# Adding the last norm's shift in a transfer instead of on GpSimd, with three output tiles and a shorter gate lead

## The chip, the core and the metric

The kernel runs on one core of a Trainium2 chip. The metric is the device time of one execution in microseconds (us). All data is float32.

## What is computed

The input `x` has 384 rows of 384 positions with 128 channels. Two layers follow each other:

```
# layer 0, a triangle product
z     = layernorm(x)
left  = (z @ Wl + bl) * sigmoid(z @ Wlg + blg)
right = (z @ Wr + br) * sigmoid(z @ Wrg + brg)
core  = einsum('bikh,bjkh->bijh', left, right)
x1    = x + sigmoid(x @ Wg + bg) * (layernorm(core) @ Wout + bout)
# layer 1, gated rows
left  = x1 @ W_left + b_left + x1 @ W_eq + b_eq
gate  = sigmoid(x1 @ W_gate + b_gate)
rsum  = sum over a row's 384 positions of (x1 @ W_right + b_right)
out   = (left * rsum * gate) @ W_out + b_out
y     = layernorm(out + x1) * ln_scale + ln_bias
```

The change concerns the very last step, `+ ln_bias`.

## The kernel before

**Three stages.** Stage 1 normalises `x`, makes `left` and `right` and writes them to a scratch tensor in DRAM. Stage 2 takes one channel `h` at a time, multiplies `left` by `right` on TensorE and writes `core_d`. Stage 3 does all that is left of layer 0 and the whole of layer 1, row by row. Stages 1 and 2 are not touched by the change.

**Slots of stage 3.** The loop runs over `t`, here called slot `t`, from 0 to 393, and each engine works through its own queue in program order. Row `i` passes through the slots as through a pipeline: in slot `i` GpSimd multiplies the core row by its scale (`cs`, L446); in slot `i+2` TensorE applies `Wout` (`pr`, L473) and VectorE forms `x1T` (L474, L476); in slot `i+3` come the two products `pg` and `pl` (L489, L490) and `u`; in slot `i+6` the row sums of four rows (`pq`, `rsum`, L463 to L465); in slot `i+7` the output product `py` (L505, L506), its statistics on VectorE (L511, L513) and, for two rows at a time, the power on GpSimd (`rs`, L515 to L520); in slot `i+9` ScalarE applies mean and scale (L527). In slot `i+10` (`D = 10`) VectorE multiplies by `-ln_scale` into the output tile `yt` (L454), which is the first VectorE instruction of its slot, and GpSimd adds `ln_bias` in place (L457).

**Quads.** An output tile holds four rows (`RG = 4`), a quad, here named by its first row. There are two output tiles (pool `p3out`), so the first L454 of quad `i+8` waits until the store of quad `i` has landed. Stores go out on SyncE's queue (SP) after the last row of a quad (L554); the last four rows are stored one by one (L549), 192 KB each instead of 768 KB.

**Fronts and their lead.** `front(f)` transposes the four tiles of row `f` of `x` (`pxt`, L431) and computes the gate of row `f-2` (`pg`, L423). Fronts run ahead of the slots:

```
while f < min(N + 2, t + max(2, A - t // 3)):
    if f == 6:
        rstd()
        load_core(0)
        load_core(RG)
    front(f)
```

With `A = 16`, sixteen fronts run before slot 0, and the lead then shrinks by one in every third slot until it is 2, in slot 42. While it shrinks, two slots in three hold a front. After that every slot holds one. `rstd()` (L395 to L414) turns the sums of stage 2 into the core's scale, writes it to DRAM and reads it back broadcast to all partitions (`rt`, L389); slot 0 needs it, and the fronts before slot 0 keep TensorE busy meanwhile.

**SyncE's queue.** All loads of stage 3 and all stores go through SP in program order. `front(f)` with `f` a multiple of 4 begins with the load of rows `f+16` to `f+19` into one of four tiles (L382): that tile holds rows `f` to `f+3`, so SP stands still until TensorE has transposed row `f+3`. In every slot that is a multiple of 4, `load_core` (L387, L389) follows, and a store L554 of quad `i` comes at the end of slot `i+13`. All of them stand behind L382 in the queue.

Of the kernel before, what the change touches and what calls it, by code (L numbers as in the profile page):

```python
# [8 lines left out]
F32 = mybir.dt.float32  # L9
AF = mybir.ActivationFunctionType  # L10
ALU = mybir.AluOpType
# [3 lines left out]
P = 128  # L15
# [4 lines left out]
def triangle_then_gated_row_kernel(ctx: ExitStack, tc: tile.TileContext, a: dict, out: bass.AP):  # L20
# [9 lines left out]
    nc = tc.nc  # L30
    x = a["x"].rearrange("b i j c -> (b i) j c")
    y = out.rearrange("b i j c -> (b i) j c")
    N, _, C = x.shape
    H = a["L0_conv_Wl"].shape[1]
    assert C == P and H == P and N % P == 0
    NB = N // P
# [2 lines left out]
    XR = 8  # L39
    KEEP = 2  # L40
    RG = 4
    A = 16

    cpool = ctx.enter_context(tc.tile_pool(name="const", bufs=1))
    dpool = ctx.enter_context(tc.tile_pool(name="scratch", bufs=1, space=DRAM))
# [4 lines left out]
    def seq(ins):  # L50

        return tc.keep_in_program_order(ins)

    def const(shape, name):
        return cpool.tile(shape, F32, tag=name, name=name)
# [18 lines left out]
    with ExitStack() as ctx2:  # L74
        lrp = ctx2.enter_context(tc.tile_pool(name="lr", bufs=2))
        inp = ctx2.enter_context(tc.tile_pool(name="p2in", bufs=3))
# [13 lines left out]
        with tc.tile_pool(name="p1x", bufs=6, side="right") as xp, \  # L90
# [71 lines left out]
            lns, lnb = const([P, C], "lns"), const([P, C], "lnb")  # L162
# [65 lines left out]
            def front(z):  # L228

                pt = tps.tile([P, 4, P], F32, tag="pt", name="pt")  # L230
                for r in range(4):
                    seq(nc.tensor.transpose(pt[:, r, :], z[:, r, :], ident))  # L232
                zt = wp.tile([P, 4, P], F32, tag="zt", name="zt")
                seq(nc.scalar.copy(zt, pt))  # L234
                return zt
# [74 lines left out]
        with tc.tile_pool(name="p2out", bufs=2, side="right", reuse_waits="tile") as op, \  # L310
# [23 lines left out]
            for h in range(H):  # L334
                fill(h + 1)
                t, rr = loaded2.pop(h), right.pop(h)
# [23 lines left out]
    with ExitStack() as ctx3:  # L360
        def pool(name, bufs, **kw):
            return ctx3.enter_context(tc.tile_pool(name=name, bufs=bufs, reuse_waits="tile", **kw))

        xip, fp, inp, op = pool("p3x", 4), pool("p3f", A + 4), pool("p3in", 3), pool("p3out", 2)
        wp, lp, sp = pool("p3w", 4), pool("p3l", 7), pool("p3s", 4)
        ps, ps2 = pool("p3ps", 4, space=PSUM), pool("p3ps2", 4, space=PSUM)

# [6 lines left out]
        cols = [slice(b * P, (b + 1) * P) for b in range(NB)]  # L374
        lnsb = lns.unsqueeze(1).to_broadcast([P, NB, C])
        lnbb = lnb.unsqueeze(1).to_broadcast([P, NB, C])
        rows, yts, pair, quad, xin, cin = {}, {}, {}, {}, {}, {}

        def load_x(i0):
# [4 lines left out]
        def load_core(i0):  # L384
            if i0 < N:
                ct = inp.tile([P, RG, N], F32, tag="ct", name="ct")
                seq(nc.sync.dma_start(out=ct, in_=core_d[i0:i0 + RG].rearrange("i h j -> h i j")))  # L387
                rt = inp.tile([P, RG, N], F32, tag="rt", name="rt")
                seq(nc.sync.dma_start(  # L389
                    out=rt.rearrange("p i j -> p (i j)"),  # L390
                    in_=rstd_d[i0:i0 + RG].rearrange("i j -> (i j)").partition_broadcast(P),
                ))
                cin[i0] = ct, rt

        def rstd():  # L395


            def temp(tag, bufs):
                return rp.tile([P, N], F32, tag=tag, name=tag, bufs=bufs)

            w = [(temp("ve", NB), temp("r", NB)) for _ in range(NB)]
            for b, (ve, r) in enumerate(w):
                m = temp("m", 2)
                seq(nc.vector.scalar_tensor_tensor(m, csum[:, b], 1.0 / (H * H), csum[:, b], ALU.mult, ALU.mult))
                seq(nc.vector.scalar_tensor_tensor(ve, csq[:, b], 1.0 / H, m, ALU.mult, ALU.subtract))
                seq(nc.vector.tensor_scalar(ve, ve, 0.0, EPS, ALU.max, ALU.add))
                seq(nc.scalar.activation(r, ve, AF.Sqrt))
            for b, (ve, r) in enumerate(w):
                m = temp("m", 2)
                seq(nc.vector.reciprocal(m, r))  # L410
                seq(nc.vector.tensor_mul(r, m, m))
                seq(nc.vector.scalar_tensor_tensor(r, r, -0.5, ve, ALU.mult, ALU.mult))
                seq(nc.vector.scalar_tensor_tensor(r, r, 1.5, m, ALU.add, ALU.mult))
                seq(nc.gpsimd.dma_start(out=rstd_d[b * P:(b + 1) * P, :], in_=r))  # L414

        D = 10
# [19 lines left out]
        def tick(t):  # L436
# [5 lines left out]
            if r:  # L442
                i = t
# [4 lines left out]
            if r:  # L448

                i = t - D  # L450
                if i % RG == 0:
                    yts[i] = op.tile([P, RG, NB, C], F32, tag="yt", name="yt")
                yt = yts[i // RG * RG][:, i % RG]
                seq(nc.vector.tensor_tensor(  # L454
                    yt, r["py"][:, :N].rearrange("p (b c) -> p b c", b=NB), lnsb, ALU.mult
                ))
                seq(nc.gpsimd.tensor_tensor(yt, yt, lnbb, ALU.add))  # L457
            m, n = divmod(t - 6, 4)
            if n == 0 and m in quad:

# [73 lines left out]
        for t in range(N + D):  # L534
# [7 lines that stand above are left out]
                f += 1  # L542
            if t % RG == 0:
                load_core(t + 2 * RG)
            tick(t)
            i = t - D
            rows.pop(i, None)
            if i >= N - RG:
                seq(nc.sync.dma_start(  # L549
                    out=y[i].rearrange("(b p) c -> p b c", p=P), in_=yts[N - RG][:, i % RG]  # L550
                ))
            elif i >= 0 and i % RG == RG - 1:
                i0 = i - RG + 1
                seq(nc.sync.dma_start(out=y[i0:i0 + RG].rearrange("i (b p) c -> p i b c", p=P), in_=yts.pop(i0)))  # L554


# [27 lines left out]
```

## Time and profile before

| what | us |
|---|---|
| median of four runs | 3465.4 (3463.13 to 3467.33) |
| the profiled execution | 3467.31 |
| its span | 3465.5 |
| stage 1, from the span's start to the first `pc` matmul | 1149 |
| stage 2, to its last `pc` matmul | 743 |
| stage 3, to the end of the span | 1573 |

Busy time in the whole span: TensorE 3408.4 us (98%), VectorE 2421.6 us (70%), ScalarE 1948.1 us (56%), GpSimd 2341.2 us (68%). The profiled execution is the span and 1.8 us around it, and it is 1.9 us longer than the median. A busy TensorE is not TensorE at its peak: a matmul's busy time also shows the pace of the clock it was granted. A releaser in square brackets is what ended an engine's idle time ahead of the instruction.

### The profile page before, as it was taken

How to read it: one execution, taken by the hardware profiler on the slowest of the kernel's cores; microseconds unless marked ns; L12 is line 12 of the kernel's file. 1: busy time of each engine (PE TensorE's matmuls, PEld its weight loads, DVE VectorE, ACT ScalarE, POOL GpSimd, SP SyncE). 2: the span in 40 equal slices, each digit the busy share in tenths (PEclk: the TensorE clock that was granted, in tenths of full speed). 3: DMA queues.
4: the chain of work that ended last, by engine and by line, in shares of the span. 5: the costliest groups of instructions: out<-in, count | busy, mean ns of one | idle time of the engine just before them, and what ended most of it. 6: DMA issues, size and time to landing. Idle time of an engine off the chain costs nothing.

```text
span 3465.5 us, 47967 instructions
## 1 busy us (share of the span) xinstructions
PE 3408.4 (98%) x13646; PEld 2107.5 (61%) x13646; DVE 2421.6 (70%) x7498; ACT 1948.1 (56%) x3815; POOL 2341.2 (68%) x4041
## 2 busy tenths in 40 slices
PE   8999999999999999999999989999999999999998
PEld 3444444444444566666665667777777777777775
DVE  5666666666666555555555778888888888888887
ACT  3344444444444333333334667777777777777776
POOL 6677777777777555555564567777777777777776
PEclk9999999999999999999999999999999999999999
DMA  3685866858765598999999655666666656565662
GB/s 95 193 232 163 230 197 198 233 162 229 199 195 151 184 284 282 282 282 284 283 284 279 200 186 186 194 200 201 196 205 192 209 188 212 185 213 187 210 210 83
DMA packets 884865, 726.00 MB, mean 209 GB/s; under 512 B 18533, under 2 KB 823017, under 8 KB 884601
## 3 DMA queue, kind: packets, MB, share of 16 engines
q1 hardware_dynamic: 882336, 720.31, 67.6%
q8 instruction: 110, 1.80, 0.2%
q10 hardware_dynamic: 2072, 2.04, 0.2%
q14 instruction: 155, 1.26, 0.1%
q0 software_dynamic: 192, 0.59, 0.0%
HBM read 437.07 MB, written 285.80 MB: 209 GB/s over the span
## 4 chain that ended last, share of the span: by engine, by line
PE 96%; DMA 2%; DVE 1%; POOL 1%; ACT 0%; issue 0%; SPq 0%; POOLq 0%; ACTq 0%; DVEq 0%
PE pr L255 29%; PE pc L340 21%; PE pr L473 7%; PE py L505 7%; PE pl L490 7%; PE pg L489 7%; PE pg L423 7%; PE pt L232 4%; PE py L506 3%; PE pxt L431 3%; DMA out_dram<-yt 1%; PE pq L463 0%; POOL rs L516 0%; DMA rt<-rstd_d 0%; ACT py L527 0%
## 5 line engine op out<-in xcount | busy, mean ns | idle before, releaser
L255 PE MATMUL pr<-wz,zt 128*128 128x512 f32 x2304 | 1040.8, 594 | 0.7 <-ACT zt L234 0.7
L340 PE MATMUL pc<-rr,lrh 128*128 128x384 f32 x2304 | 743.3, 486 | 1.5 <-issue 1.5
L257 ACT ACTIVATE sg<-pr 128x512 f32<-128x512 f32 x576 | 344.2, 598 | 645.6 <-PE pr L255 332.3
L255 PEld LDWEIGHTS pr<-wz,zt 128*128 128x128 f32 x2304 | 416.6, 191 | 415.1 <-issue 414.1
L259 DVE TENSOR_TENSOR lr<-pr,sg 128x512 f32<-128x512 f32 x576 | 398.5, 692 | 377.7 <-ACT sg L257 377.7
L340 PEld LDWEIGHTS pc<-rr,lrh 128*128 128x128 f32 x2304 | 451.8, 196 | 293.2 <-issue 2.3
L527 ACT ACTIVATE py<-py,nm,rs 128x128 f32<-128x128 f32 x1152 | 495.5, 430 | 124.3 <-POOL rs L520 94.6
L223 POOL TENSOR_SCALAR z<-xt,rs,sh 128x128 f32<-128x128 f32 x1152 | 497.6, 448 | 0.6 <-POOL z L223 0.4
L505 PEld LDWEIGHTS py<-wo,u 128*128 128x128 f32 x2304 | 378.7, 191 | 107.2 <-ACT py L527 3.2
L349 DVE TENSOR_TENSOR csum<-csum,ct 128x1152 f32<-128x1152 f32 x128 | 192.0, 1500 | 345.6 <-ACT ct L346 345.6
L505 PE MATMUL py<-wo,u 128*128 128x128 f32 x2304 | 404.4, 275 | 4.8 <-ACT py L527 3.0
L457 POOL TENSOR_TENSOR yt<-yt,lnb 128x384 f32<-128x384 f32 x384 | 383.3, 998 | 19.8 <-DVE yt L454 19.8
L346 ACT COPY ct<-pc 128x1152 f32<-128x1152 f32 x128 | 143.3, 1120 | 450.1 <-PE pc L340 446.2
L326 POOL COPY rr<-lrh 128x768 f32<-128x768 f32 x128 | 171.2, 1337 | 323.6 <-DMA lrh<-lr_d 284.3
L446 POOL TENSOR_TENSOR cs<-ct,rt 128x384 f32<-128x384 f32 x384 | 383.5, 999 | 7.8 <-PE pxt L431 3.8
L511 DVE BATCH_NORM_STATS2 st<-py 128x6 f32<-128x128 f32 x1152 | 266.6, 287 | 111.3 <-PE py L506 111.2
L423 PE MATMUL pg<-xT,mat_L_conv_Wg 128*128 128x384 f32 x768 | 314.8, 492 | 13.6 <-DVE rsum L465 8.9
L473 PE MATMUL pr<-cs,wc 128*128 128x384 f32 x768 | 320.2, 499 | 0.0
L490 PE MATMUL pl<-x1T,mat_L_conv_W_left 128*128 128x384 f32 x768 | 312.5, 489 | 2.4 <-DVE rsum L465 2.3
L506 PE MATMUL py<-ident,x1T 128*128 128x128 f32 x1152 | 314.6, 273 | 0.0
L489 PE MATMUL pg<-x1T,mat_L_conv_W_gate 128*128 128x384 f32 x768 | 312.3, 488 | 2.3 <-ACT gT L425 1.4
L474 DVE SCALAR_TENSOR_TENSOR pr<-pr,bz,gT 128x384 f32<-128x384 f32 x384 | 240.1, 625 | 106.5 <-PE pr L473 106.5
(88 smaller groups left out, 5040.3 us busy)
## 6 DMA issues: line engine op xcount, KB each, us to landing
lr_d<-lr SPq DMA_DIRECT2D x128, 1024.0 KB, 9.3
lrh<-lr_d SPq DMA_DIRECT2D x128, 768.0 KB, 7.7
xt<-in_x_dram SPq DMA_DIRECT2D x144, 512.0 KB, 7.0
xt<-in_x_dram SPq DMA_DIRECT2D x96, 768.0 KB, 5.0
ct<-core_d SPq DMA_DIRECT2D x96, 768.0 KB, 6.7
rt<-rstd_d SPq DMA_DIRECT2D x96, 768.0 KB, 8.2
out_dram<-yt SPq DMA_DIRECT2D x95, 768.0 KB, 9.2
core_d<-ct SPq DMA_DIRECT2D x125, 576.0 KB, 8.8
```

What stands on the lines that cost most here:

```text
L223: seq(nc.gpsimd.tensor_scalar(z[:, r, :], xt[:, rr, :], rs[:, rr:rr + 1], sh[:, rr:rr + 1], ALU.mult, ALU.add))
L255: seq(nc.tensor.matmul(pr[:, r, :], lhsT=zt[:, 2 * half + r, :], rhs=wz, start=True, stop=True))
L259: seq(nc.vector.tensor_tensor(t[:, :, i0:i0 + 2, :], pr[:, :, :2 * H].rearrange("k i (h s) -> k h i s", s=2), sg.rearrange("k i (h s) -> k ...
L340: seq(nc.tensor.matmul(pc[:, ib, :N], lhsT=t[:, kb, ib * P:(ib + 1) * P, 0], rhs=rr[:, kb], start=(kb == 0), stop=(kb == NB - 1),))
L423: seq(nc.tensor.matmul(pg[:, :N], lhsT=wg0, rhs=r["xT"], start=True, stop=True))
L446: seq(nc.gpsimd.tensor_tensor(cs, ct[:, i % RG], rt[:, i % RG], ALU.mult))
L473: seq(nc.tensor.matmul(pr[:, :N], lhsT=wc, rhs=r["cs"], start=True, stop=True))
L489: seq(nc.tensor.matmul(pg2[:, :N], lhsT=wgate, rhs=r["x1T"], start=True, stop=True))
L490: seq(nc.tensor.matmul(pl[:, :N], lhsT=wleft, rhs=r["x1T"], start=True, stop=True))
L505: seq(nc.tensor.matmul(py[:, s], lhsT=r["u"][:, s], rhs=r["wo"], start=True, stop=False))
L506: seq(nc.tensor.matmul(py[:, s], lhsT=r["x1T"][:, s], rhs=ident, start=False, stop=True, is_transpose=True))
L527: seq(nc.scalar.activation(py[:, s], py[:, s], AF.Identity, bias=nm[:, n, b:b + 1], scale=rs[:, n, b:b + 1]))
```

## The change

The add of `ln_bias` (L457) leaves GpSimd for all rows but the last four. In its place a constant tile `lnb4`, which holds `ln_bias` twelve times per partition, is filled once by GpSimd before stage 3 begins, and in slot `i+14` GpSimd's queue issues a transfer that adds `lnb4` to the whole output tile of quad `i` in place (`accum_op`). The store of quad `i` moves from slot `i+13` to slot `i+17`, and waits for that transfer. The output pool gets a third tile, and `lnb4` is as large as one of them; `A` falls from 16 to 12, which frees four tiles of each of the two kinds in pool `p3f`.

```diff
-    A = 16
+    A = 12
...
-        xip, fp, inp, op = pool("p3x", 4), pool("p3f", A + 4), pool("p3in", 3), pool("p3out", 2)
+        xip, fp, inp, op = pool("p3x", 4), pool("p3f", A + 4), pool("p3in", 3), pool("p3out", 3)
+        cp = pool("p3c", 1)
...
+        lnb4 = cp.tile([P, RG, NB, C], F32, name="lnb4")
+        seq(nc.gpsimd.tensor_copy(
+            lnb4.rearrange("p i b c -> p (i b) c"), lnb.unsqueeze(1).to_broadcast([P, RG * NB, C])
+        ))
...
-                seq(nc.gpsimd.tensor_tensor(yt, yt, lnbb, ALU.add))
+                if i >= N - RG:
+                    seq(nc.gpsimd.tensor_tensor(yt, yt, lnbb, ALU.add))
...
                 seq(nc.sync.dma_start(
                     out=y[i].rearrange("(b p) c -> p b c", p=P), in_=yts[N - RG][:, i % RG]
                 ))
-            elif i >= 0 and i % RG == RG - 1:
-                i0 = i - RG + 1
+            i0 = t - D - RG
+            if 0 <= i0 < N - RG and i0 % RG == 0:
+                seq(nc.gpsimd.dma_start(
+                    out=yts[i0].rearrange("p i b c -> p (i b c)"), in_=lnb4.rearrange("p i b c -> p (i b c)"),
+                    accum_op=ALU.add,
+                ))
+            i0 = t - D - RG - 3
+            if 0 <= i0 < N - RG and i0 % RG == 0:
                 seq(nc.sync.dma_start(out=y[i0:i0 + RG].rearrange("i (b p) c -> p i b c", p=P), in_=yts.pop(i0)))
```

## The prediction

> **What bounds the kernel.** I read the page's busy shares first (TensorE 98%), then busy time by stretches of stage 3. Columns: stretch, length, then busy time of TensorE, its weight loads, VectorE, ScalarE, GpSimd, then granted clock, DMA share, GB/s.
>
> ```profile
> 1930.00:2000.00 70.00, 66.07 (x327) 46.01 (x326) 53.12 (x188) 44.45 (x104) 43.52 (x62) 0.98 0.46 151
> 2000.00:2400.00 400.00, 391.24 (x1998) 279.06 (x1997) 321.22 (x1116) 294.38 (x680) 285.38 (x395) 0.99 0.60 194
> 2400.00:2800.00 400.00, 400.00 (x2071) 288.05 (x2069) 329.57 (x1136) 307.06 (x707) 291.23 (x406) 1.00 0.62 201
> 3420.00:3465.50 45.50, 28.61 (x154) 21.26 (x152) 27.37 (x106) 25.86 (x61) 28.22 (x42) 0.84 0.24 70
> ```
>
> From about 2095 to 3420 TensorE has no idle time: a quad takes 15.85 us (the chain's marks at 2412.18, 2428.03 and 2443.88), and GpSimd stands at 73%. So the adds that leave GpSimd (380 of 998 ns, 379 us) buy nothing there. What can move is the first 200 us of stage 3 and the last 30. The waits between 1880 and 2100 (total, times, longest) name the cause in the first part:
>
> ```profile
> DVE yt L454 <- DMA out_dram<-yt: 17.1, 5, 4.6
> PE pg L423 <- DVE rsum L465: 8.9, 3, 3.1
> PE pl L490 <- DVE rsum L465: 2.3, 2, 2.0
> ```
>
> VectorE waits five times for an output tile whose store has not landed; `rsum`, next in its queue, is late, and TensorE stands. TensorE's timeline (start, length, instruction, idle before it) has these five, and the start of slot 2:
>
> ```profile
> 1917.52 0.49 PE L431 MATMUL pxt<-ident,xt 128*128 128x128 f32 x3
> 1917.85 1.46 PE L473 MATMUL pr<-cs,wc 128*128 128x384 f32 x4
> ...
> 1977.75 0.91 PE L423 MATMUL pg<-xT,mat_L_conv_Wg 128*128 128x384 f32 x2 [2.94 <-DVE rsum L465]
> ...
> 2009.16 0.91 PE L490 MATMUL pl<-x1T,mat_L_conv_W_left 128*128 128x384 f32 x2 [0.33 <-DVE rsum L465]
> ...
> 2028.12 0.91 PE L423 MATMUL pg<-xT,mat_L_conv_Wg 128*128 128x384 f32 x2 [2.84 <-DVE rsum L465]
> ...
> 2059.80 0.91 PE L490 MATMUL pl<-x1T,mat_L_conv_W_left 128*128 128x384 f32 x2 [1.96 <-DVE rsum L465]
> ...
> 2079.00 1.65 PE L423 MATMUL pg<-xT,mat_L_conv_Wg 128*128 128x384 f32 x2 [3.09 <-DVE rsum L465]
> ```
>
> SP's queue shows why stores are late: each burst begins when L382 is released, and the store goes out behind it.
>
> ```profile
> 1996.60 0.37 SPq L382 DMA_DIRECT2D xt<-in_x_dram  x1
> 1997.07 0.70 SPq L387 DMA_DIRECT2D ct<-core_d  x1
> 1997.82 0.95 SPq L389 DMA_DIRECT2D rt<-rstd_d  x1
> 1998.87 0.48 SPq L554 DMA_DIRECT2D out_dram<-yt  x1
> ...
> 2019.22 0.37 SPq L382 DMA_DIRECT2D xt<-in_x_dram  x1
> 2019.69 0.71 SPq L554 DMA_DIRECT2D out_dram<-yt  x1
> ...
> 3453.77 0.37 SPq L554 DMA_DIRECT2D out_dram<-yt  x1
> ```
>
> **Step 1, what the five waits cost now.** From the lead's formula, front `f` runs in a known slot, so the release of each L382, and of the store behind it, is a slot number. With A = 16 the stores of quads 0, 8, 12, 20, 24 leave in slots 17, 23, 29, 35, 41, and their tiles are wanted in slots 18, 26, 30, 38, 42. These are the five waits. Idle: 2.94 + 0.33 + 2.84 + 1.96 + 3.09 = 11.2. After a gap TensorE may run slower: from 1977.75 the next five groups took 4.96 us, where the same groups take 2.93 at full pace, so 2.0 lost; 2079.00 to the `pr` at 2087.01 took 8.0, where a front (0.98) and a slot (3.91) make 4.9, so 3.1; by the same reckoning 0.5 after 2028.12 and 0.1 after 2059.80. Together 5.7. The waits cost 16.9 us.
>
> The granted clock shows it: 0.78 from 2070 to 2085. A gap of 2.94 us was enough for it and one of 2.84 nearly free. The Trainium skill ("TensorE: Matmul & The Clock Gate", Part 1) says that the clock halves after an idle window of about 3.4 us; by that rule all five gaps would cost their idle time alone, 11.2 us. The rows decide: 16.9.
>
> **Step 2, what is left of them.** With A = 12 every front of the shrinking lead comes in the slot in which the front four rows earlier came, and the lead reaches 2 in slot 30, not 42. The store of quad `i` is now queued in slot `i+17`, and its tile is wanted in slot `i+22`: both move by four slots, so the third tile by itself gives the store no more time. The same reckoning: quad 0 leaves in slot 17, wanted in 22 (free); quad 4 in 23, wanted in 26; quad 8 in 29, wanted in 30; from quad 12 on, five or four slots, as in the steady part, where there was no wait. Two waits remain.
>
> Slot 26 is the kind that cost 0.33 and 2.1. There the transfer of quad 8, issued in slot 22, runs beside the burst and holds up the store behind it by 2.5 to 4.9 us (step 4): 0.3 to 6, taken 4.5. Slot 30 is the kind that cost 3.3 (2.8 to 6 by the clock), taken 3.3. Left 7.8; gain 16.9 - 7.8 = **9.1 us** (4.9 to 13.8).
>
> **Step 3, the shorter lead.** TensorE's sixteen fronts ended at 1917.85, when `cs` of row 0 had been ready for over a microsecond:
>
> ```profile
> 1915.58 3.87 POOL L446 TENSOR_TENSOR cs<-ct,rt 128x384 f32<-128x384 f32 x4
> ```
>
> Four fronts fewer (0.98 each) end at 1913.95. `cs` begins after the scale's third write on GpSimd (1915.01), which A does not move, and takes 0.97. TensorE stands from 1913.95 to 1916.6: **2.65 us lost**, since the four fronts are made up later, in slots 30 to 42. Slow clock after it: by the gap of 2.84 up to 0.5, by that of 2.94 2.0. Taken 2.7, bounds 0 and 4.7. `lnb4`'s copy falls into GpSimd's idle 20.2 us before 1906.55; with 1.34 us for 768 elements (L326) it needs about 2.7 us, while VectorE's sums there have 3.2 us of waiting for ScalarE. Nothing; without that cover up to 2.7 us, all ahead of `rt`.
>
> **Step 4, the added transfer, steady part.** Per quad the DMA engines work 0.62 x 15.85 = 9.8 us for four transfers of 768 KB, 2.46 each; 6.0 are free. No accumulating transfer is in the trace. It moves as many bytes into the tile, so 2.46 is its floor, and since it must also read the tile I take twice that, 4.9, as upper bound and value. Both fit into 6.0.
>
> The Trainium skill ("Collectives: The Full Stack", on the fold count) says that a reducing transfer runs at half a copy's rate because of its two source reads. That speaks against the change; an estimate by that rule, two copies' time, would be no less than the value taken, and no row here shows it.
>
> The store in the burst now lands some 9.1 + 4.9 = 14 us after its issue, about 2.5 us behind the release, and its tile is wanted 18 to 20 us after the release: 2 to 3 us to spare. On GpSimd the issue costs about 0.56 us (L414, 0.54 to 0.80); behind it stand `cs` and the next `rs`, which idles 1.8 to 2.0 us before each pair, where 2 of 4 us of adds are gone too. SP's next loads stand behind the store's wait for the transfer, issued four slots earlier: nothing unless it takes over 15.85 us. Steady part: **0** (no gain, since TensorE is full).
>
> **Step 5, the end.** Before, the store of quad 376 left at 3453.77 and the last row's add ended at 3462.49; its 192 KB take 2.0, and the span ends at 3465.5, 1.0 later. Now quad 376's transfer is issued behind `rs` of the last pair (3458.16) and its 768 KB store is the very last instruction on SP. Issue by 3458.9; landing between 4.4 us (a 768 KB store here) and 8.8 (twice that), then 4.4 for the store and 1.0: 3468.7 to 3473.1, so +3 to +8, taken **+4.5**. A few adds fewer in the chain of the end give back below 0.5.
>
> **Sum.** -9.1 + 2.7 + 4.5 = -1.9 on the profiled 3467.3: 3465.4. The median is 1.9 below that execution, so **3463.5** there. The ends add up to -10.8 and +7.8: 3455 to 3473 is this case's own range.
>
> **Rivals.** *The waits go:* the transfer does not hold up the store in slot 26, quad 8 loses little, the end is short. 13.8 gained, 0 to 1 lost at the start, 3 at the end: about 3456. For it: both 0.33 and 2.1 stand in the trace. Against it: quad 8's store leaves one slot before it is wanted. 0.17. *The losses return:* slow clock at the start, 6 us at each wait, +8 at the end: 3473. 0.15. *The DMA engines fill:* above 6.0 us per transfer (2.4 times a copy) the burst no longer fits into a quad, stores land late in every quad, and TensorE waits for VectorE as in slot 18. At three times a copy (7.4) a quad grows by 1.4 us; 84 quads between 2100 and 3430 make +115, so 3580. For it: the DMA share is 0.62 already and the transfer reads twice. Against it: its rows are 6 KB long in each partition, while most packets here are below 2 KB. 0.20. *Nothing moves:* the waits shift by four slots and all come back: 3465. 0.04. My forecast has 0.44.
>
> **Chances.** 0.2% is 7 us, about what a measurement of this kernel tells from no change. Faster: nearly all of the first rival and the edge of the forecast, 0.19. Slower: the filled DMA engines, most of the returning losses and the edge, 0.36. Within: 0.45. The range 3453 to 3485 leaves out most of the filled engines (0.16) and little below.
>
> **What would show it.** Right: L454 waits twice for stores before 2100; TensorE idle about 2.6 us before the first `pr`; TensorE at 400.00 of 400 in the steady part with a DMA share of 0.8 to 0.95; the span ends with quad 376's store. Wrong: a quad longer than 15.85 us; L454 waiting for `out_dram` after 2200; five waits again.

## The result and the profile after

The changed kernel takes 3469.5 us (median of 42 runs, 3466.3 to 3472.4) against 3465.6 us (60 runs of the kernel before): a ratio of 1.0011, with a 95% interval of 1.0007 to 1.0015. It is 3.9 us slower, inside the forecast range and inside 0.2%, but on the other side of the forecast, which had 1.9 us faster. Its profiled execution has a span of 3469.2 us, 3.7 us longer than before.

Busy time by stretches of stage 3 (columns as before):

```profile
1930.00:2000.00 70.00, 69.02 (x350) 48.86 (x349) 57.71 (x205) 48.02 (x111) 34.67 (x52) 1.00 0.59 179
2400.00:2800.00 400.00, 399.96 (x2069) 287.85 (x2069) 329.56 (x1136) 306.56 (x707) 220.62 (x330) 1.00 0.86 250
3420.00:3469.20 49.20, 28.84 (x152) 22.09 (x150) 26.82 (x105) 25.42 (x61) 21.33 (x34) 0.79 0.56 137
```

The steady part is as forecast: TensorE is full, GpSimd falls from 73% to 55%, the DMA share rises from 0.62 to 0.86, and nearly every quad still takes 15.85 us. The waits from 1880 to 2110, and below the dots the one from 2110 to 3400:

```profile
DVE yt L459 <- DMA out_dram<-yt: 10.4, 3, 5.6
...
PE pl L496 <- DVE rsum L471: 4.8, 1, 4.8
...
PE pg L428 <- DVE rsum L471: 3.1, 1, 3.1
PE pr L479 <- POOL cs L451: 2.8, 1, 2.8
...
DVE yt L459 <- DMA out_dram<-yt: 4.5, 10, 0.6
```

Two waits that reach TensorE are left of five, in slots 26 and 30, as the slot numbers said. But they are larger than their forerunners. TensorE's timeline:

```profile
1895.55 1.65 PE L428 MATMUL pg<-xT,mat_L_conv_Wg 128*128 128x384 f32 x2 [1.02 <-ACT xT L438]
...
1918.59 2.59 PE L479 MATMUL pr<-cs,wc 128*128 128x384 f32 x4 [2.77 <-POOL cs L451]
...
2010.14 1.65 PE L496 MATMUL pl<-x1T,mat_L_conv_W_left 128*128 128x384 f32 x2 [4.81 <-DVE rsum L471]
...
2031.33 1.03 PE L428 MATMUL pg<-xT,mat_L_conv_Wg 128*128 128x384 f32 x2 [3.05 <-DVE rsum L471]
```

The gap in slot 26 was 0.33 us before and is 4.81 now, and the doubled times after it (1.65 for a pair that takes 0.81 to 0.91 at full pace) show the slow clock. Marks make the loss countable: the `pq` matmuls of slots 26 and 30 are 21.30 us apart, those of slots 30 and 34 are 20.93 apart. Without the waits (kernel `e5_after_load_late` below) the same stretches take 14.21 and 15.85. So the two cost 7.1 and 5.1 us. The marks of slots 26, 30 and 34, first in the changed kernel, then in that one:

```profile
2003.66 0.28 PE L469 MATMUL pq<-tot,mat_L_conv_W_right 128*128 128x4 f32 x2
...
2024.96 0.28 PE L469 MATMUL pq<-tot,mat_L_conv_W_right 128*128 128x4 f32 x2
...
2045.89 0.28 PE L469 MATMUL pq<-tot,mat_L_conv_W_right 128*128 128x4 f32 x2
```

```profile
2004.12 0.28 PE L469 MATMUL pq<-tot,mat_L_conv_W_right 128*128 128x4 f32 x2
...
2018.33 0.28 PE L469 MATMUL pq<-tot,mat_L_conv_W_right 128*128 128x4 f32 x2
...
2034.18 0.28 PE L469 MATMUL pq<-tot,mat_L_conv_W_right 128*128 128x4 f32 x2
```

SP's queue and GpSimd's issue at the first of the two waits:

```profile
1993.10 0.37 SPq L387 DMA_DIRECT2D xt<-in_x_dram  x1
1993.57 0.71 SPq L392 DMA_DIRECT2D ct<-core_d  x1
1994.34 0.61 SPq L394 DMA_DIRECT2D rt<-rstd_d  x1
1995.05 0.59 SPq L568 DMA_DIRECT2D out_dram<-yt  x1
```

```profile
1995.32 0.92 POOL L562 DMA_DIRECT2D yt<-lnb  x1
```

Quad 8's transfer is issued 0.3 us after quad 4's store, and that store, last of a burst, lands after 14.2 us; before, the one wanted in slot 26 took 9.4. From issue to landing of the transfer and the store in the changed kernel (11.8 and 14.2), then of the one store before:

```profile
DMA to landing us min/median/max: 11.8/13.0/14.2
```

```profile
DMA to landing us min/median/max: 9.4/9.4/9.4
```

The end of the program, SP's last store and GpSimd's drains there (instructions of the program's end; times in ns, shortest, median, longest), then the drains in the kernel before:

```profile
3463.24 0.37 SPq L568 DMA_DIRECT2D out_dram<-yt  x1
```

```profile
L594 POOLq DRAIN  x3: 40/93/6937, 3460.3 to 3468.7; - x3
```

```profile
L580 POOLq DRAIN  x3: 40/102/1362, 3461.5 to 3465.3; - x3
```

Quad 376's store is last, as forecast, and its data moves until about 3467.6. But GpSimd also drains, for 6.9 us from its last add on, from 3460.3 to 3467.2; in the kernel before the longest drain took 1.36 us.

### The profile page after: what moved, and what is told of

Same layout as the page of the kernel before. It is cut to its first block, busy times and chain, and to the rows that moved or that the text cites. A ratio compares the mean times of both kernels' runs of the same rounds, so it can differ in the third digit from the quotient of the medians.

```text
span 3469.2 us, 47770 instructions
## 1 busy us (share of the span) xinstructions
PE 3410.6 (98%) x13646; PEld 2110.6 (61%) x13646; DVE 2417.0 (70%) x7498; ACT 1947.9 (56%) x3815; POOL 2079.1 (60%) x3757
## 3 DMA queue, kind: packets, MB, share of 16 engines
q0 software_dynamic: 13872, 75.31, 10.7%
## 4 chain that ended last, share of the span: by engine, by line
PE 97%; DMA 1%; DVE 1%; ACT 1%; POOL 0%; issue 0%; POOLq 0%; SPq 0%; ACTq 0%; DVEq 0%
PE pr L255 29%; PE pc L340 21%; PE pr L479 7%; PE py L511 7%; PE pl L496 7%; PE pg L495 7%; PE pg L428 7%; PE pt L232 4%; PE py L512 4%; PE pxt L436 4%; DMA out_dram<-yt 1%; PE pq L469 0%; ACT py L533 0%; POOL rs L522 0%; DMA col_L_conv_norm_b<-in_L_conv_norm_b_dram 0%
## 5 line engine op out<-in xcount | busy, mean ns | idle before, releaser
L349 DVE TENSOR_TENSOR csum<-csum,ct 128x1152 f32<-128x1152 f32 x128 | 183.6, 1434 | 352.3 <-ACT ct L346 352.3
L521 POOL TENSOR_SCALAR rs<-mv 128x6 f32<-128x6 f32 x192 | 38.3, 200 | 622.7 <-DVE mv L519 595.4
L451 POOL TENSOR_TENSOR cs<-ct,rt 128x384 f32<-128x384 f32 x384 | 401.7, 1134 | 5.4 <-PE pr L479 5.3
L498 ACT ACTIVATE g<-pg,col_L_conv_b_gate 128x384 f32<-128x384 f32 x384 | 223.0, 581 | 156.3 <-PE pg L495 155.2
```

Of the source, the lines that this page charges most:

```text
L451: seq(nc.gpsimd.tensor_tensor(cs, ct[:, i % RG], rt[:, i % RG], ALU.mult))
```

## The experiments

Each time stands against runs of the kernel before on the same chip; differences in us are ratios times 3465.

**1. The lead alone** (`e1_lead12`).

```diff
-    A = 16
+    A = 12
```

> The kernel before with A = 12 alone. Theory (slot numbers set the waits): the waits in slots 18, 26 and 30 stay, those in slots 38 and 42 go, which gives back 2.1 + 6.2 = 8.3 us; the shorter lead costs between 2.7 us (2.65 idle) and 5.6 (the profiled execution of the changed kernel was that much behind once the four fronts are counted). Net -2.7 to -5.6. Rival (the shorter lead only costs, and its waits just come earlier, all five of them): +2.7 to +5.6.

Measured: 3463.5, ratio 0.9993 (0.9985 to 1.0002), -2.4. The trace has waits in slots 18, 26 and 30 and a clean 15.85 us per quad from slot 34 on. The slot reckoning holds, and no slowing by the shorter lead shows here, since it also ends the waits earlier. The stretch from slot 30 to 34 takes 20.88 us, 5.0 above 15.85, without any accumulating transfer.

**2. The third tile where the store stays in slot `i+13`** (`e2_lead12_tile3`).

```diff
-    A = 16
+    A = 12
...
-... pool("p3out", 2)
+... pool("p3out", 3)
```

> The kernel before with A = 12 and three output tiles; the shift is still added on GpSimd and the store still goes out after slot i+13. Theory: with the store at its old place the third tile gives every store at least four slots, so all five waits go: -16.9, and the lead costs +2.7 to +5.6: net -11 to -14. In the changed kernel the third tile is used up by the four slots that the accumulating transfer takes. Rival (the third tile brings little, as the waits come from the transfers' time and not from the slot of their release): as A = 12 alone, within 2 us.

Measured: 3452.4, ratio 0.9959 (0.9946 to 0.9973), -14. No wait for a store is left. So the third tile takes away the three waits that experiment 1 still has, 11.8 us by the two ratios and 9.8 by the marks of slots 6 and 46; the changed kernel spends it on the four slots that its store is moved back.

**3. The end without quad 376's transfer** (`e3_last8_gpsimd`; the same bound, two quads instead of one, also ends the transfers and the stores of slot `i+17`).

```diff
-                if i >= N - RG:
+                if i >= N - 2 * RG:
...
+            if i == N - RG - 1:
+                i0 = N - 2 * RG
+                seq(nc.sync.dma_start(out=y[i0:i0 + RG]..., in_=yts.pop(i0)))
```

> The changed kernel, but the last eight rows and not the last four get their shift on GpSimd, and quad 376 is stored right after its last row in slot 389. Theory: the end of the changed kernel is set by quad 376's transfer and store, 43.3 us from the mark at 3425.9 to the end of the span against 39.0 before, so this takes back 4 us: -4 against the changed kernel, about 0 against the kernel before. Rival (the cost lies in the steady part, where VectorE waits ten times for a store, 4.5 us in total): the time stays at that of the changed kernel, +4.

Measured: 3468.2, ratio 1.0009 (1.0000 to 1.0018): only about 1 us back of the 4 expected. The trace shows why. GpSimd's last add and its drains:

```profile
3457.98 0.99 POOL L463 TENSOR_TENSOR yt<-yt,lnb 128x384 f32<-128x384 f32 x1 [0.29 <-DVE yt L459]
```

```profile
L597 POOLq DRAIN  x3: 40/93/6834, 3457.9 to 3465.6; - x3
```

No data moves after 3461, yet the span ends at 3465.9, 1.1 us after the long drain (3457.9 to 3464.8). The late store and the drain lie beside each other in the changed kernel, so taking away the one leaves the other.

**4. The load behind the transposes** (`e4_load_late`).

```diff
-                if f % RG == 0:
-                    load_x(f + 4 * RG)
                 pxt = bank("pxt")
                 for b, s in enumerate(cols):
                     seq(nc.tensor.transpose(...))
+                if f % RG == RG - 1:
+                    load_x(f + 1 + 3 * RG)
```

> The kernel before (A = 16, two output tiles, shift on GpSimd) with the load of rows f+16 to f+19 queued after the transposes of row f+3 that free its tile, instead of ahead of those of row f, so that SP does not stand still in front of stores. Theory: the five waits come from stores that stand behind that load; all five go, -15 to -17. Rival (two tiles are too few while slots are short: a store needs 8 to 11 us, and the tile is wanted 5 slots, 18 us, after its last row): the waits become smaller but at least those in slots 18, 30 and 42 stay, -5 or less.

Measured: 3449.3, ratio 0.9954 (0.9942 to 0.9967), -16. With two tiles, lead 16 and no accumulating transfer, VectorE waits for no store at all. The five waits were head-of-line waits in SP's queue. This is also the fastest version of all, 20 us below the changed kernel. Its trace has the slow first front as well, without any part of the change:

```profile
1895.71 1.65 PE L423 MATMUL pg<-xT,mat_L_conv_Wg 128*128 128x384 f32 x2 [1.01 <-ACT xT L433]
```

**5. The changed kernel with the late load** (`e5_after_load_late`, the same edit).

> The changed kernel with the load of rows f+16 to f+19 queued after the transposes of row f+3. Theory: its two waits (slots 26 and 30) cost 7.4 and 5.1 us of its 3.9 us loss and stand behind that load; they go: -12 against the changed kernel, 3457 to 3459; what is left above the kernel before with the same move (3449.3) is 9 us: four fronts of lead 3.9, the end 4.3, the steady part 0.8. Rival (the wait in slot 26 comes from the accumulating transfer beside the burst): slot 26 keeps half its loss, 3461 to 3463.

Measured: 3455.8, ratio 0.9971 (0.9959 to 0.9982), -10, which is 14 us below the changed kernel. Both waits go, so the transfer alone does not make them: it makes the first of them larger, and SP's queue starts both. The rest above experiment 4 is 5.9 us.

**6. The lead alone without waits** (`e6_load_late_lead12`, experiment 4 with A = 12).

> The kernel before with the late load (no waits for stores) and A = 12, against the same with A = 16 (3449.3). It prices the lead alone. Theory: the slow clock after TensorE's gap ahead of the first core row eats the head start, so the lead costs all four fronts, 4 x 0.98 = 3.9: 3453. The prediction's term: 2.7: 3452. Rival (more, as the profiled execution suggests, 5.6): 3455.

Measured: 3452.0, ratio 0.9959 (0.9947 to 0.9972), against 0.9954 with A = 16: +1.7. Each of the two intervals reaches about 4 us to either side, so the times alone cannot tell 2.7 from 3.9 or 5.6. The traces can: the stretch from slot 6 to slot 46 grows from 148.95 to 151.80, 2.85 us, near the prediction's 2.7 and not the 5.6 that the changed kernel's profile had suggested.

**7. Quad 8 without its transfer** (`e7_quad8_gpsimd`).

```diff
-                if i >= N - RG:
+                if i >= N - RG or i // RG == 2:
...
-            if 0 <= i0 < N - RG and i0 % RG == 0:
+            if 0 <= i0 < N - RG and i0 != 2 * RG and i0 % RG == 0:
                 seq(nc.gpsimd.dma_start(
```

> The changed kernel, but quad 8 gets its shift from GpSimd and not from a transfer. Theory: the transfer of quad 8, issued 0.3 us after quad 4's store, holds up that store beyond slot 26; without it slot 26 loses 1 to 2.5 us and not 7.4: -5 to -6.5 against the changed kernel, 3463 to 3464.5. Rival (the store is late through its place in SP's queue alone): the loss stays, 3469.

Measured: 3464.6, ratio 0.9991 (0.9982 to 1.0000). One transfer out of 95 is worth 5.5 us by the medians beside their kernels before (-1.7 against +3.9) and 6.9 by the ratios. The gap in slot 26 is 1.00 us, the store lands after 10.0, and the stretch from slot 26 to 30 takes 15.47 and not 21.30:

```profile
2003.99 0.91 PE L496 MATMUL pl<-x1T,mat_L_conv_W_left 128*128 128x384 f32 x2 [1.00 <-DVE rsum L471]
```

```profile
DMA to landing us min/median/max: 10.0/10.0/10.0
```

**8. Transfers for the first 48 quads only** (`e8_accum_first_half`, experiment 3 with `N // 2` in place of `N - 2 * RG` in the condition on the add and on the transfer).

> The kernel in which the last eight rows get their shift on GpSimd and quad 376 is stored early (3468.2), with the transfer used for the first 48 quads only; rows 192 and up get their shift on GpSimd. In the former the span ends 7.95 us after GpSimd's last work, with a drain of 6.8 us there, against 1.4 in the kernel before. Theory (the drain clears what recent transfers of GpSimd's queue left behind): drain 1.4, the end 3.9 us earlier, 3464 to 3465. Rival (the drain goes by the number of such transfers in the program or by their being there at all): drain 4 to 7 us, 3466 to 3468.

Measured: 3466.9, ratio 1.0003 (0.9994 to 1.0012). The drain is 5.29 us, 750 us after the last transfer. It does not go by how recent they are.

**9. A second transfer per quad** (`e9_second_transfer`).

```diff
-    A = 12
+    A = 10
...
+                seq(nc.gpsimd.dma_start(
+                    out=side.rearrange("p i b c -> p (i b c)"), in_=lnb4.rearrange("p i b c -> p (i b c)"),
+                    accum_op=ALU.add,
+                ))
```

> The changed kernel with a second accumulating transfer of 768 KB per quad, of the same constant tile into a tile that nobody reads (A = 10 makes room for it, which costs two fronts, about 2 us). It tests the capacity of the DMA engines. Theory: one such transfer takes 3.9 us of the 16 engines (10.7% of 3469.2 us, by 95), so the share of 0.86 rises to 1.1: 13.6 + 3.9 = 17.5 us of work in a quad of 15.85; quads grow to about 17.5 and the time by 90 x 1.65 = 150 us, to about 3620. Rival (the busy share overstates, since it already reads above 1.1 in bursts, and the engines still have room): below 3490.

Measured: 3643.0 (two runs), ratio 1.0516 (1.0474 to 1.0557), +179. The steady part:

```profile
2400.00:2800.00 400.00, 370.76 (x1828) 264.63 (x1827) 290.97 (x1003) 271.68 (x626) 214.75 (x313) 0.96 0.99 265
```

The DMA engines are full (0.99), TensorE waits, and its clock falls now and then. A quad takes 17.7 us in the mean of slots 46 to 382, where 17.5 were expected. The busy share is a true measure of room here, and the rival of the filled DMA engines had the right mechanism and a threshold that one transfer per quad does not reach.

**10. Transfers for the first 12 quads only** (`e10_accum_12_quads`).

> As the kernel with transfers for the first 48 quads, but for the first 12 only. It reads the length of GpSimd's drain at the end: 1.36 us with the three scale writes alone, 5.29 with 48 transfers more, 6.9 with 95 more. Theory (the drain goes by the number of GpSimd's transfers in the program, less than in proportion): 2 to 4 us. Rival (it is a fixed price of having such transfers at all, plus a little for each): 4 to 5 us.

Measured: 3464.5, ratio 0.9996 (0.9985 to 1.0007). The longest drain of experiments 10, 8 and 9:

```profile
L597 POOLq DRAIN  x3: 40/102/2344, 3460.0 to 3463.8; - x3
...
L597 POOLq DRAIN  x3: 40/93/5286, 3460.8 to 3466.6; - x3
...
L600 POOLq DRAIN  x3: 40/102/11573, 3621.9 to 3635.0; - x3
```

With 12, 48, 95 and 190 accumulating transfers the drain is 2.3, 5.3, 6.9 and 11.6 us, with none 1.36: it goes by their number, 82 ns more for each up to 48 and less beyond. What it does in that time is not shown.

## Why the prediction was wrong, by its steps

Experiments 4, 6 and 5 and the changed kernel form a chain in which each link is one or two steps of the sum: -15.9 (all waits taken away), +1.7 (the lead), +4.2 (third tile, transfer and end, no waits), +13.8 (the waits of the changed kernel come back). That makes +3.8. By the intervals each link is known to 4 to 6 us only; what tells the steps apart is the traces.

| step | forecast | by the runs | by the traces |
|---|---|---|---|
| 1, the five waits of before | -16.9 | -15.9 | -18.1 |
| 2, what is left of them | +7.8 | +13.8 | +12.2 |
| 3, the shorter lead | +2.7 | +1.7 | +2.9 |
| 4, the steady part | 0 | together +4.2 | +0.8 |
| 5, the end | +4.5 | | +4.3 |
| sum | -1.9 | +3.8 | +2.1 |

The first `pq` of stage 3 also comes 1.7 us later in the changed kernel's profile, which is no part of the table; with it the traces give 3.8, where the spans differ by 3.7.

**Step 2 failed, in its size.** Which waits go and which stay was right, slot by slot, and so was the reason that the third tile gives the store no time. Slot 26 was put at 4.5 and cost 7.1. Against experiment 7, which leaves out this one transfer, the store landed 4.2 us later (14.2 and not 10.0), within the 2.5 to 4.9 that the prediction gave the transfer, and TensorE's gap grew from 1.00 to 4.81. After the gap comes the slow clock (0.50 from 2010 to 2014), 2.3 us more, which the 4.5 did not contain. The transfer's part is 5.8 of the 7.1 by the marks. Slot 30 was put at 3.3 by its forerunner, whose gap of 2.84 us had brought almost no slow clock; with 3.05 us it came, and the wait cost 5.1. That is not the transfer's doing, as experiment 1 has 5.0 there without one. The 2.84 was an exception and no safe length: in the profiles here nine gaps of 2.52 to 2.78 us were followed by the slow clock and one of 2.60 was not. Taking the exception's value was the gamble, and the bound of 6 beside each wait held 5.1 but not 7.1.

**Step 1** had the right cause: experiment 4 leaves no wait by moving one instruction in SP's queue.

**Step 3** had the right size, 2.7 against 2.9, in part by luck. The prediction counted 2.65 of the four fronts' 3.9 us as lost in the gap ahead of the first `pr` and put next to nothing for the slow clock. The gap came (2.77), and the slow clock with it: the first four `pr` take 2.59 us, where before they took 1.46. By slot 6 the whole head start is gone: in experiment 4 and the changed kernel the first `pq` comes 35.44 us after the transposes at 1894.15 and 1893.99. But the four fronts then cost 2.9 and not 3.9 when they are made up, because with A = 16 those slots had lost about 1 us of their own: two of their stretches take 15.60 and 14.21 us in experiment 4, and 15.85 less one and two fronts of 0.98 would be 14.87 and 13.89.

The first core row comes 1.95 us later than before in the profile; 0.34 of that is the end of stage 2, and 1.6 the slow clock after the very first fronts (the 1.65 at 1895.55, where before it was 0.91). Of the twelve profiles seven have this and five do not: with A = 16 one each, with the transfer five and two, with A = 12 and no transfer one and two. Nothing here ties it to the change, and one profiled execution is not the median.

**Step 4**: a transfer takes 3.9 us of the engines (10.7% of the span, by 95), between the floor of 2.46 and the 4.9 taken. It fits, as argued, with less to spare than reckoned. The tile is wanted 15.9 us after the release and not 18 to 20 (released at 2315.80, wanted at 2331.6), and a quad's accumulating transfer is issued three slots ahead of its store (`i+14` and `i+17`), not four. So VectorE waits for a store ten times, 4.5 us in all, nine of them after 2200, where the prediction had called such waits a sign of being wrong. Little of it reaches TensorE: five of 84 quads are longer, by 0.8 us together, and with the late load (experiment 5) none is. The half rate that the Trainium skill ("Collectives: The Full Stack", on the fold count) gives for the reducing transfers of a ring is not what this one shows: 3.9 is 1.6 times the 2.46 of the other transfers here, which are in part of shorter rows. GpSimd's issue takes 0.93 us, not 0.56.

**Step 5** had the right size with half of the cause. The late store was seen, the drain beside it was not. In the changed kernel the store's data ends 0.4 us after the drain, and experiment 3 shows that the drain alone holds the end nearly as long.

The rival of the returning losses (+7.8) was nearest in mechanism: its 6 us at each wait come to 12, where 12.2 were measured, and its slow clock at the start came; its 8 us at the end did not (4.3). It had 0.15.

## What to carry to other kernels

When a tile is added and a step is put between its last write and its store, count in the program's own slots when the store can leave and when the tile is wanted: here both moved by four, and the tile bought the store no time. Before buying a buffer, look at what stands ahead of the late transfer in its queue; moving one load behind the work that frees its tile gave 16 us with no memory at all. Price a wait of TensorE with the slow clock behind it as soon as the gap may pass the 2.5 us at which it came here, and do not put a large transfer into the stretch where a store is already the last to land.

## What the runs showed of the hardware that was not expected

- GpSimd's drain at the end of the program grows with the number of accumulating transfers that it issued: 1.36 us with none, 2.3 with 12, 5.3 with 48, 6.9 with 95, 11.6 with 190.
- In the first 200 us of stage 3, experiment 9 left out, TensorE's clock fell after 17 of 19 gaps of 2.5 to 3.4 us (not after 2.84 in the kernel before and 2.60 in experiment 1). It also fell after 0.88 and 1.02 us with 0.55 us of work between them in seven of twelve profiles. The Trainium skill ("TensorE: Matmul & The Clock Gate", Part 1) speaks of an idle window of about 3.4 us; these gaps are shorter. The page also calls that window free-running; that could make what a gap meets differ from place to place, but it does not explain gaps shorter than the window, and no run here shows the window.
- An accumulating transfer of 768 KB from tile to tile moved 197 GB/s with nothing beside it at a DMA share near 1.0 (3446 to 3448 in experiment 3), against 290 for a store (3465 to 3467 in the changed kernel).
- Right behind the issue of such a transfer two `cs` on GpSimd take 2.24 us together, where they take 1.95 otherwise.
